# A graph network layer on one core: silu on ScalarE, and two kinds of tiles taken off GpSimd's gathers

## The chip, the cores and the metric

The kernel runs on one core of one Trainium2 chip. The metric is the device time of one execution in microseconds. The engines are called by the profile's names: PE (TensorE), DVE (VectorE), ACT (ScalarE), POOL (GpSimd) and SP (SyncE).

## The reference

There are 12500 nodes of 64 features and 412500 edges of 32 features, sorted by receiver (`dst`).

```
h = maximum(layernorm(x), 0)
m = concat(h[src], h[dst], edge_attr)                 # 160 wide, one row an edge
messages   = silu(m @ W1 + b1) @ W2 + b2              # 64 wide
att_logits = silu(m @ Wa1 + ba1) @ Wa2 + ba2          # one number an edge
att        = softmax(att_logits, axis=0)              # over all edges
agg        = segment_sum(messages * att, dst)
out        = x + silu(concat(h, agg) @ Wu1 + bu1) @ Wu2 + bu2
```

## The kernel before

**Tiles.** Edges are cut into tiles of 128 (`EP`), and 8 tiles (`K`) make a group; there are 403 groups (`NG`). The products of the first layers are split in three: a table `ts_d` in device memory holds, for each node as a sender, its 128 values (64 for the attention, 64 for the message); a table `tr_d` holds the same for receivers with the biases; the edge's own part is multiplied on PE. All of them are held at half size (the weights are halved), so that `tanh` of the sum gives `silu` of its double: silu(2z) = z (1 + tanh z).

**One group.** `load(g)` starts the fetches: for each tile one indirect DMA on POOL (L513) gathers the 128 senders' rows of `ts_d` into the tile `gs`; two DMAs on SP (L534) fetch a window of `tr_d` into one of three `wins`; each fourth group SP also fetches edges and receivers' numbers (`eo`, `dbs`). DVE compares the receivers' numbers (L538), and PE multiplies (L542) into the PSUM tile `pe`, 128 x 8 x 128. `begin(g)` adds `pe` and `gs` on DVE (L553) into `gs` and takes tanh on ACT (L556). `end(g)` multiplies on DVE: message (L566), attention (L572), times `wa2` (L574), and sums to a logit for each edge (L577). Four groups form a batch; `top` and `weigh` take the batch's largest logit, keep the running maximum `nmax`, and make the weights `p` with Exp on ACT (L610) and the correction `scale` of older sums with a second Exp (L607). `by_node(g)` builds for each tile a 128 x 40 matrix of weights by receiver (L620, eight instructions a group), PE sums messages with it (L626), ACT copies the sums out (`out_of`, L632), PE projects them (L637), and `put` adds them to the running sums at the window's place (L651, L655, L658).

**Columns.** In every second group from 8 to 390 (`EVERY`, 192 groups) the last tile isn't gathered. The nodes' features lie transposed on the chip (`hT`), and ACT copies, one instruction an edge, the 4-byte column of each of the 128 senders (L483) at an address taken from a register; `burst(g, k)` does 32 of them twice a group, each after a load of 32 registers (L479). `columns` writes `cols`, L547 masks the wrong half by the node's parity (`half`, fetched by SP), and one more product on PE (L548) adds the tile into `pe`.

**Order.** The loop over `g` runs `begin(g)`, parts of the summing up of a group five before (`sum_up`), `burst(g, 0)`, `load(g + 2)`, `numbers(g + 6)`, more summing up, `end(g)`, `burst(g, 1)`, and, where a batch begins, `weigh` of the batch before. `pin` puts an instruction behind the one traced before it on its engine; the register loads of `columns` and of `put` aren't pinned. In the groups 16 to 118 the loop also makes the nodes' own share of the last layer (`tile_bias`, L314 and L323; `tile_rest`). Gathers have 7 buffers, `pe` has 3. The last 12 groups have no columns, and the last 7 are batches of one group.

Of the kernel before, what the change touches and what calls it, by code (L numbers as in the profile page):

```python
# [44 lines left out]
WIDE = 128  # L45
EPS = 1e-5
# [313 lines left out]
def one_pass(tc, n_edges, v):  # L360
# [17 lines left out]
    with ExitStack() as ctx:  # L378
# [43 lines left out]
        with tc.tile_pool(name="work2", bufs=2) as work2, \  # L422
                tc.tile_pool(name="small", bufs=3) as small, \
                tc.tile_pool(name="pre_ps", bufs=AHEAD + 1, space=PSUM) as pre_ps, \
                tc.tile_pool(name="one_ps", bufs=1, space=PSUM) as one_ps:
            pes, gss, lgs, ps_, psums, sps, pps, ees, mts, nums, cols = ({} for _ in range(11))
# [12 lines left out]
            chosen = {g: i for i, g in enumerate(picks)}  # L439
            hT8 = v["hT"].rearrange("d b p -> d (b p)").bitcast(U8)  # L440
            sets = [(i, min(P, len(picks) - i)) for i in range(0, len(picks), P)]
# [3 lines left out]
            def places():  # L445

                num, low, near = (small.tile([P, len(sets), EP], t, name=n, bufs=1)
                                  for t, n in ((I32, "num"), (I32, "low"), (F32, "near")))
                pin(nc.vector.memset(num, 0))
                for k, (i, n) in enumerate(sets):  # L450
                    e = (picks[i] * K + K - 1) * EP
                    nc.sync.dma_start(num[:n, k, :], bass.AP(
                        tensor=v["src_row"].tensor, offset=v["src_row"][:, e:].offset,
                        ap=[[EVERY * K * EP, n], [1, EP]]))
# [8 lines left out]
                for k, (i, n) in enumerate(sets):  # L463
                    nc.sync.dma_start(par_d[k * P:k * P + n, :], low[:n, k, :])
# [3 lines left out]
            def numbers(g):  # L468
                if g in chosen:
                    n = nums[g] = small.tile([P, EP], I32, name="half", bufs=3)  # L470
                    row = par_d[chosen[g]:chosen[g] + 1, :]
                    nc.sync.dma_start(n, bass.AP(tensor=row.tensor, offset=row.offset, ap=[[0, P], [1, EP]]))
                    cols[g] = small.tile([P, EP], F32, name="cols", bufs=3)

            def columns(g, first, n):
                if g not in chosen:
                    return
                to, i = cols[g].bitcast(U8), chosen[g]
                _, regs = nc.values_load_multi_w_load_instructions(  # L479
                    spots[i % P:i % P + 1, i // P, first:first + n], engines=[ENG.Activation],  # L480
                    min_val=HT_AT, max_val=HT_AT + 2 * NP - 4, skip_runtime_bounds_check_because=WHY)
                for i in range(n):
                    pin(nc.scalar.copy(to[:, 4 * (first + i):4 * (first + i) + 4],  # L483
                                       hT8[:, bass.ds(regs[i] - HT_AT, 4)]))

            def burst(g, k):
# [6 lines left out]
            tr_w = bass.AP(tensor=tr_d.tensor, offset=tr_d.offset,  # L493
                           ap=[[C, NP + WR - SHIFT], [SHIFT * C, 2], [1, C]])

            def registers(g, engine, at, base=base_sb, top=NP - 1):
                n = min(NQ, NG + (base is not base_sb) - g)
                _, regs = nc.values_load_multi_w_load_instructions(
                    base[0:1, g:g + n], engines=[engine], min_val=0, max_val=top,
                    skip_runtime_bounds_check_because=WHY)  # L500
                for i in range(n):
                    at[g + i] = regs[i]

            def load(g):

                t = g * K
                if g % NQ == 0:
                    registers(g, ENG.SP, at_sp)
                full = gather.tile([P, K, C], F32, name="gs")
                gs = gss[g] = full[:EP]  # L510
                for j in range(K - (g in chosen)):
                    rows = WIDE if j in (2, 3) else EP
                    nc.gpsimd.indirect_dma_start(  # L513
                        out=full[:rows, j, :], out_offset=None, in_=ts_d[:, :],
                        in_offset=bass.IndirectOffsetOnAxis(ap=src_full[:rows, t + j:t + j + 1], axis=0))
# [17 lines left out]
                for r in range(2):  # L533
                    nc.sync.dma_start(win[r * R:(r + 1) * R, :, r, :],  # L534
                                      tr_w[bass.ds(at_sp[g], R), :, :])
# [14 lines left out]
            def begin(g):  # L550

                n = K - (g in chosen)
                pin(nc.vector.tensor_tensor(gss[g][:, :n, :], pes[g][:, :n, :], gss[g][:, :n, :], ALU.add))  # L553
                if n < K:
                    pin(nc.vector.tensor_copy(gss[g][:, n, :], pes[g][:, n, :]))
                pin(nc.scalar.activation(pes[g], gss[g], AF.Tanh))  # L556

            def end(g, then=None):

                s = batch[g]  # L560
                if g == starts[s]:
                    lgs[s] = small.tile([EP, B * K], F32, name="lg")
                gs, th = gss.pop(g), pes.pop(g)

                def message():
                    pin(nc.vector.scalar_tensor_tensor(acts[g % ACTS][:, :, 0:U], th[:, :, U:C], 1.0,  # L566
                                                       gs[:, :, U:C], op0=ALU.add, op1=ALU.mult))

                if g < NG - 1:
                    message()  # L570
                att = th[:, :, 0:U]
                pin(nc.vector.scalar_tensor_tensor(att, th[:, :, 0:U], 1.0, gs[:, :, 0:U],  # L572
                                                   op0=ALU.add, op1=ALU.mult))
# [3 lines left out]
                pin(nc.vector.tensor_reduce(lgs[s][:, k:k + K], att, AX.X, ALU.add))  # L577
# [4 lines left out]
                if g == NG - 1:  # L582
                    message()

            def top(s):

                n = size[s] * K
                lg = lgs[s]
# [10 lines left out]
            def weigh(s):  # L599
# [5 lines left out]
                fall = small.tile([P, 1], F32, name="fall")  # L605
                pin(nc.vector.tensor_tensor(fall, nmax[:, s + 1:s + 2], nmax[:, s:s + 1], ALU.subtract))
                pin(nc.scalar.activation(scale[:, s:s + 1], fall, AF.Exp))  # L607
                p = ps_[s] = small.tile([EP, B * K], F32, name="p")
                psum = small.tile([EP, 1], F32, name="psum")
                pin(nc.scalar.activation(p[:, :n], lgs.pop(s)[:, :n], AF.Exp, bias=nmax[:EP, s + 1:s + 2],  # L610
                                         accum_out=psum))
                psums[s] = psum

            def by_node(g):

                k = (g - starts[batch[g]]) * K
                wt = work2.tile([EP, K, W], F32, name="wt")
                p = ps_[batch[g]]
                for j in range(K):
                    pin(nc.vector.tensor_scalar(wt[:, j, :], iota_w[:EP, j // H, :],  # L620
                                                dloc[:, g * K + j:g * K + j + 1],
                                                p[:, k + j:k + j + 1],
                                                op0=ALU.is_equal, op1=ALU.mult))
# [94 lines left out]
            for g in range(NG):  # L718
# [6 lines left out]
                begin(g)  # L725
                if more and g < NG - 1:
# [10 lines left out]
                if g + AHEAD < NG:  # L737
                    load(g + AHEAD)
                numbers(g + 6)
# [384 lines left out]
```

## Time and profile before

| | |
|---|---|
| runs | 3901.23, 3902.33, 3901.85 us; median 3901.85 |
| the profiled execution | 3904.89 us, span of its instructions 3903.1 us |
| busy share of the span | DVE 80%, ACT 76%, POOL 74%, PE 61% |
| mean granted clock of PE | 0.642 |
| indirect DMAs on POOL | 3032, 198.90 MB by that queue |
| DMA | 391.30 MB, mean 100 GB/s |

A row of a group reads: line, engine, operation, output <- inputs, shape, count | busy us in all, mean ns of one | idle us of the engine just ahead of them, and what ended most of it. "Issue" is idle time in which the engine waited for nothing that the profile shows. A row of a stretch reads: the stretch, its length, then for PE, PEld (weight loads), DVE, ACT and POOL the busy us and the count, then PE's clock, the DMA engines' share and GB/s; with one line alone it has one engine only. A row of one line's records reads: line, engine (with a q: its queue, for loads, register work and DMA issues), operation, count, then shortest, median and longest ns, and the first and last start in us.

### The profile page before, as it was taken

What the parts mean: (1) busy time and instruction counts of PE and PEld (TensorE: products, weight loads), DVE (VectorE), ACT (ScalarE), POOL (GpSimd) and SP (SyncE); (2) the same over time, 40 slices, a digit from 0 to 9 for tenths busy, and PEclk for the clock granted to TensorE, in tenths of its full rate; (3) what the DMA queues carried; (4) which work ended last, traced back from release to release, by engine and by line L of the source; (5) the groups of instructions that cost most, each with busy time, mean ns of one, the idle gap of its engine ahead of it and who ended that gap; (6) DMA issues with size and microseconds to landing.
All of it is one profiled execution on the core that took longest, in us unless ns stands there. A gap on an engine that the chain in (4) does not pass through costs nothing. (4 is left out here: it accounts for less than half of the span.)

```text
span 3903.1 us, 72226 instructions
## 1 busy us (share of the span) xinstructions
PE 2368.6 (61%) x11368; PEld 1927.2 (49%) x11368; DVE 3115.4 (80%) x8929; ACT 2954.1 (76%) x25797; POOL 2888.6 (74%) x3057
## 2 busy tenths in 40 slices
PE   6566656666666666665665656556565565555655
PEld 5454444454445554554444545445444454444545
DVE  6888787878788888887877877778777777877887
ACT  2887777777778888887877777878877878878712
POOL 3777777777777777777777777777777777777774
PEclk8766566666666657666666666666666666666666
DMA  7433334333433333333333333333333333333343
GB/s 280 114 104 94 102 100 106 94 104 99 107 93 97 97 97 91 94 97 94 87 97 85 97 93 89 97 86 97 93 88 97 86 96 91 90 97 86 95 116 86
DMA packets 228304, 391.30 MB, mean 100 GB/s; under 512 B 72369, under 2 KB 155762, under 8 KB 214770
## 3 DMA queue, kind: packets, MB, share of 16 engines
q0 software_dynamic: 97024, 198.90, 19.5%
q1 hardware_dynamic: 130802, 187.73, 17.9%
q14 instruction: 385, 3.15, 0.3%
q8 instruction: 93, 1.52, 0.2%
HBM read 360.52 MB, written 25.82 MB: 99 GB/s over the span
## 5 line engine op out<-in xcount | busy, mean ns | idle before, releaser
L513 POOL DMA_INDIRECT gs<-ts_d,src_sb x3032 | 2871.4, 947 | 973.1 <-issue 844.2
L483 ACT COPY cols<-hT 128x4 uint8 x24576 | 2415.5, 189 | 595.2 <-issue 594.2
L542 PE MATMUL pe<-wins,eo 128*128 128x256 f32 x3224 | 1470.7, 630 | 846.4 <-DVE eo L538 619.9
L542 PEld LDWEIGHTS pe<-wins,eo 128*128 128x128 f32 x3224 | 964.4, 316 | 1145.4 <-DVE eo L538 708.6
L620 DVE TENSOR_SCALAR wt<-iota_w,dloc,p 128x40 f32<-128x40 f32 x3224 | 726.9, 323 | 1.8
L553 DVE TENSOR_TENSOR gs<-pe,gs 128x1024 f32<-128x1024 f32 (+1 forms) x403 | 467.0, 1159 | 325.7 <-DMA gs<-ts_d,src_sb 303.3
L626 PE MATMUL sp<-wt,acts 128*65 128x40 f32 x6448 | 621.9, 268 | 4.6 <-DVE wt L620 3.5
L626 PEld LDWEIGHTS sp<-wt,acts 128*65 128x65 f32 x6448 | 586.0, 183 | 11.4 <-DVE wt L620 6.2
L556 ACT ACTIVATE pe<-gs 128x1024 f32<-128x1024 f32 x403 | 410.6, 1019 | 215.9 <-DVE gs L553 125.3
L637 PEld LDWEIGHTS mt<-ss,w2u 65*128 65x128 f32 x806 | 201.7, 281 | 330.4 <-issue 291.9
L637 PE MATMUL mt<-ss,w2u 65*128 65x40 f32 x806 | 183.7, 322 | 255.5 <-DVE gm L603 221.4
L566 DVE SCALAR_TENSOR_TENSOR acts<-pe,gs 128x512 f32<-128x512 f32 x403 | 277.6, 689 | 21.6 <-ACT pe L556 12.2
L574 DVE TENSOR_TENSOR pe<-pe,w_all 128x512 f32<-128x512 f32 x403 | 281.8, 699 | 13.5
L572 DVE SCALAR_TENSOR_TENSOR pe<-pe,gs 128x512 f32<-128x512 f32 x403 | 280.3, 696 | 10.5
L596 PE MATMUL mt<-ident,mx 128*128 128x128 f32 x107 | 46.7, 437 | 396.4 <-DVE sums L655 375.9
L577 DVE TENSOR_REDUCE lg<-pe 128x8 f32<-128x512 f32 x403 | 276.7, 687 | 10.5
L538 DVE TENSOR_SCALAR eo<-dbs,bj 64x256 f32<-64x256 int32 x806 | 275.5, 371 | 9.2
L596 PEld LDWEIGHTS mt<-ident,mx 128*128 128x128 f32 x107 | 19.2, 179 | 408.3 <-issue 404.5
L658 DVE COPY stand<-nmax 64x40 f32 x806 | 159.0, 197 | 3.4 <-issue 0.3
L547 DVE SCALAR_TENSOR_TENSOR cols<-half,cols 128x128 f32<-128x128 int32 x192 | 67.1, 349 | 100.6 <-ACT cols L483 98.5
L651 DVE SCALAR_TENSOR_TENSOR sums<-sums,scale,mt 64x40 f32 x214 | 54.4, 254 | 110.9 <-PE mt L637 107.4
L548 PEld LDWEIGHTS pe<-stack,cols 128*128 128x128 f32 x384 | 121.7, 317 | 32.5
(126 smaller groups left out, 957.6 us busy)
## 6 DMA issues: line engine op xcount, KB each, us to landing
eo<-in_edge_dram SPq DMA_DIRECT2D x100, 512.0 KB
dbs<-in_dst_row_dram SPq DMA_DIRECT2D x200, 256.0 KB
gs<-ts_d,src_sb POOLq DMA_INDIRECT x3032
wins<-tr_d SPq DMA_DIRECT2D x806, 32.0 KB
half<-par_d SPq DMA_DIRECT2D x192, 64.0 KB
ts_d<-ts SPq DMA_DIRECT2D x5, 896.0 KB
tr_d<-tr SPq DMA_DIRECT2D x5, 896.0 KB
hT_d<-hT SPq DMA_DIRECT2D x7, 448.0 KB
```

What stands on the lines that cost most here:

```text
L483: pin(nc.scalar.copy(to[:, 4 * (first + i):4 * (first + i) + 4], hT8[:, bass.ds(regs[i] - HT_AT, 4)]))
L513: nc.gpsimd.indirect_dma_start(out=full[:rows, j, :], out_offset=None, in_=ts_d[:, :], in_offset=bass.IndirectOffsetOnAxis(ap=src_full[:ro ...
L542: pin(nc.tensor.matmul(pe[:, 2 * q:2 * q + 2, :], eo[:, q * EP:(q + 1) * EP], win[:, q // 2, :, :], start=True, stop=q < H - 1 or g not in ...
L553: pin(nc.vector.tensor_tensor(gss[g][:, :n, :], pes[g][:, :n, :], gss[g][:, :n, :], ALU.add))
L556: pin(nc.scalar.activation(pes[g], gss[g], AF.Tanh))
L566: pin(nc.vector.scalar_tensor_tensor(acts[g % ACTS][:, :, 0:U], th[:, :, U:C], 1.0, gs[:, :, U:C], op0=ALU.add, op1=ALU.mult))
L572: pin(nc.vector.scalar_tensor_tensor(att, th[:, :, 0:U], 1.0, gs[:, :, 0:U], op0=ALU.add, op1=ALU.mult))
L574: pin(nc.vector.tensor_tensor(att, att, wa2[:EP, None, :].to_broadcast([EP, K, U]), ALU.mult))
L577: pin(nc.vector.tensor_reduce(lgs[s][:, k:k + K], att, AX.X, ALU.add))
L620: pin(nc.vector.tensor_scalar(wt[:, j, :], iota_w[:EP, j // H, :], dloc[:, g * K + j:g * K + j + 1], p[:, k + j:k + j + 1], op0=ALU.is_equ ...
L626: pin(nc.tensor.matmul(sp, acts[g % ACTS][:, j, :], wt[:, j, :], start=j == 0, stop=j == K - 1))
L637: pin(nc.tensor.matmul(pp, w2u.rearrange("s h u -> s (h u)"), sps.pop(g), start=True, stop=True))
```

## The change

- `begin(g)` adds the gathered rows into `pe` in PSUM, and ACT makes silu(2z) from there with two instructions, one for the attention half into a tile `att` and one for the message half straight into `acts`. The two products on DVE (L566, L572) go, and so does the copy of the column tile out of PSUM.
- Exp isn't used in the loop any more. `weigh` makes the weights from Tanh: with t = tanh(x/32), ((1 + t)/(1 - t)) = exp(x/16); three squarings on DVE give exp(x/2), and Square on ACT with its accumulator gives exp(x) and the sum. The correction `scale` rides along as a 33rd column.
- `by_node` builds the eight matrices of a group in two instructions (one comparison, one product of 128 x 320).
- In every eighth group (11, 19, ... 387: 48 groups) the last tile's columns are copied by DVE: `vcolumns` loads eight registers twice a group, `spare_columns` issues the copies, 16 a group, so that a tile takes eight groups.
- In every eighth group (15, 23, ... 383: 47 groups) the last tile is fetched row by row by SP: `fetch` loads 16 registers and issues 16 DMAs of 512 bytes a group; the byte addresses are the senders' numbers shifted left by 9 on DVE, and `begin` adds the tile `lone` with an addition of its own.
- The windows' addresses are given in bytes (`base_by`), shifted once ahead of the loop.

```diff
+ROWS = 16
+ROW0 = 6
+VTURN = 8
+VRES = (3,)
+VSTART = 0
+VLATER = 11
+VBUFS = 2
...
+            vpicks = [g for g in range(VSTART + VLATER, NG - 12) if g % VTURN in VRES]
...
+            def vcolumns(g, part):
+                at, end = (i * EP * len(VRES) // (2 * VTURN) for i in (2 * (g - VSTART) + part,
+                                                                        2 * (g - VSTART) + part + 1))
+                end = min(end, len(vpicks) * EP)
+                while 0 <= at < end:
+                    t, first = vpicks[at // EP], at % EP
+                    n = min(end - at, EP - first)
+                    if first == 0:
+                        cols[t] = small.tile([P, EP], F32, name="vcols", bufs=VBUFS)
+                    loads, regs = spots_of(t, first, n, ENG.DVE)
+                    for one in loads:
+                        pin(one)
+                    to = cols[t].bitcast(U8)
+                    waiting.extend((to[:, 4 * (first + i):4 * (first + i) + 4], regs[i]) for i in range(n))
+                    at += n
+
+            def spare_columns(n=None):
+                for to, reg in waiting[:n]:
+                    pin(nc.vector.tensor_copy(to, hT8[:, bass.ds(reg - HT_AT, 4)]))
+                waiting[:] = waiting[len(waiting) if n is None else n:]
...
+            for i in range(NG):
+                g = ROW0 + (EP * (i + 1) - 1) // ROWS + 2
+                if g < NG - 12:
+                    fetched[g] = i
...
+            def fetch(g):
...
+                    loads, regs = nc.values_load_multi_w_load_instructions(
+                        ids[i][0:1, first:first + n], engines=[ENG.SP], min_val=0, max_val=(NP - 1) * 4 * C,
+                        skip_runtime_bounds_check_because=WHY)
+                    for one in loads:
+                        pin(one)
+                    for k in range(n):
+                        pin(nc.sync.dma_start(to[first + k:first + k + 1, :].bitcast(U8),
+                                          ts8[bass.ds(regs[k], 4 * C)][None, :]))
...
-                for j in range(K - (g in chosen)):
+                for j in range(K - (g in chosen) - (g in fetched)):
...
-                n = K - (g in chosen)
-                pin(nc.vector.tensor_tensor(gss[g][:, :n, :], pes[g][:, :n, :], gss[g][:, :n, :], ALU.add))
-                if n < K:
-                    pin(nc.vector.tensor_copy(gss[g][:, n, :], pes[g][:, n, :]))
-                pin(nc.scalar.activation(pes[g], gss[g], AF.Tanh))
+                n = K - (g in chosen) - (g in fetched)
+                pe, gs = pes[g], gss.pop(g)
+                pin(nc.vector.tensor_tensor(pe[:, :n, :], pe[:, :n, :], gs[:, :n, :], ALU.add))
+                if g in fetched:
+                    pin(nc.vector.tensor_tensor(pe[:, n, :], pe[:, n, :], lone.pop(g)[:EP], ALU.add))
+                del pes[g]
+                att = atts[g] = silus.tile([P, K, U], F32, name="att")[:EP]
+                pin(nc.scalar.activation(att, pe[:, :, 0:U], AF.Silu, scale=2.0))
+                pin(nc.scalar.activation(acts[g % ACTS][:, :, 0:U], pe[:, :, U:C], AF.Silu, scale=2.0))
...
-                pin(nc.scalar.activation(scale[:, s:s + 1], fall, AF.Exp))
+                lg = lgs.pop(s)
+                pin(nc.vector.tensor_scalar(lg[:, n:n + 1], nmax[:, s:s + 1], -1.0, None, op0=ALU.mult))
+                part = small.tile([P, 1], F32, name="part")
+                pin(nc.vector.tensor_scalar(part, nmax[:, s + 1:s + 2], 1.0 / 32, None, op0=ALU.mult))
+                t, d = (small.tile([P, B * K + 1], F32, name=k)[:, :n + 1] for k in ("t", "d"))
+                pin(nc.scalar.activation(t, lg[:, :n + 1], AF.Tanh, bias=part, scale=1.0 / 32))
+                spare_columns()
+                pin(nc.vector.tensor_scalar(d, t, -1.0, 1.0, op0=ALU.mult, op1=ALU.add))
+                spare_columns(3)
+                pin(nc.vector.reciprocal(d, d))
+                spare_columns(3)
+                pin(nc.vector.scalar_tensor_tensor(t, t, 1.0, d, op0=ALU.add, op1=ALU.mult))
+                for _ in range(3):
+                    spare_columns(3)
+                    pin(nc.vector.tensor_tensor(t, t, t, ALU.mult))
                 p = ps_[s] = small.tile([EP, B * K], F32, name="p")
                 psum = small.tile([EP, 1], F32, name="psum")
-                pin(nc.scalar.activation(p[:, :n], lgs.pop(s)[:, :n], AF.Exp, bias=nmax[:EP, s + 1:s + 2],
-                                         accum_out=psum))
+                pin(nc.scalar.activation(p[:, :n], t[:EP, :n], AF.Square, accum_out=psum))
+                spare_columns(3)
+                pin(nc.vector.tensor_tensor(scale[:, s:s + 1], t[:, n:n + 1], t[:, n:n + 1], ALU.mult))
...
-                for j in range(K):
-                    pin(nc.vector.tensor_scalar(wt[:, j, :], iota_w[:EP, j // H, :],
-                                                dloc[:, g * K + j:g * K + j + 1],
-                                                p[:, k + j:k + j + 1],
-                                                op0=ALU.is_equal, op1=ALU.mult))
+                at = dloc[:, g * K:(g + 1) * K].rearrange("p (r h) -> p r h", h=H)
+                pin(nc.vector.tensor_tensor(wt.rearrange("p (r h) w -> p r h w", h=H),
+                                            iota_w[:EP, :, None, :].to_broadcast([EP, 2, H, W]),
+                                            at[:, :, :, None].to_broadcast([EP, 2, H, W]), ALU.is_equal))
+                pin(nc.vector.tensor_tensor(wt, wt, p[:, k:k + K, None].to_broadcast([EP, K, W]), ALU.mult))
...
                 begin(g)
+                vcolumns(g, 0)
...
                     load(g + AHEAD)
+                fetch(g)
                 numbers(g + 6)
...
+                spare_columns()
+                vcolumns(g, 1)
                 end(g)
                 burst(g, 1)
                 if batch[g] and g == starts[batch[g]]:
                     weigh_upto(batch[g] - 1)
+                spare_columns()
```

More of the change, by code (lines that the diff above doesn't have):

```diff
@@ L488, in burst @@
                     columns(g + 3 + i, *SLOTS[EVERY - 1 - i][k])
-            at_sp, at_lo, at_hi, bus, rest = {}, {}, {}, {}, {}
[L493 to L497, printed above, removed]
+            fetched = {}
+            for i in range(NG):
+                g = ROW0 + (EP * (i + 1) - 1) // ROWS + 2
+                if g < NG - 12:
+                    fetched[g] = i
@@ new lines, in one_pass, with ask, scaled @@
+            order = list(fetched)
+            ids, lone = {}, {}
+            ts8 = ts_d.rearrange("n f -> (n f)").bitcast(U8)
+            def ask(i):
+                if i < len(order):
+                    g = order[i]
+                    e = (g * K + K - 1 - (g in chosen)) * EP
+                    ids[i] = small.tile([1, EP], I32, name="ids", bufs=2)
+                    nc.sync.dma_start(ids[i], v["src_row"][:, e:e + EP])
+            def scaled(i):
+                if i < len(order):
+                    pin(nc.vector.tensor_scalar(ids[i], ids[i], 9, None, op0=ALU.logical_shift_left))
@@ new lines, in fetch @@
+            def fetch(g):
+                at = (g - ROW0) * ROWS
+                end = min(at + ROWS, len(order) * EP)
+                if g == ROW0 - 3:
+                    ask(0)
+                if g == ROW0 - 2:
+                    scaled(0)
+                while 0 <= at < end:
+                    i, first = at // EP, at % EP
+                    n = min(end - at, EP - first)
+                    if first < ROWS:
+                        ask(i + 1)
+                    if EP // 2 <= first < EP // 2 + ROWS:
+                        scaled(i + 1)
+                    if first == 0:
+                        lone[order[i]] = small.tile([P, C], F32, name="lone", bufs=2)
+                    to = lone[order[i]]
+                    loads, regs = nc.values_load_multi_w_load_instructions(
[6 more added lines that the diff above has]
+                                          ts8[bass.ds(regs[k], 4 * C)][None, :]))
+                    at += n
@@ new lines, in one_pass, with registers @@
+            at_sp, at_lo, at_hi, bus, rest = {}, {}, {}, {}, {}
+            row = 4 * C
+            tr8 = tr_d.bitcast(U8)
+            tr_w = bass.AP(tensor=tr8.tensor, offset=tr8.offset,
+                           ap=[[1, (NP - 1) * row + 1], [row, R], [SHIFT * row, 2], [1, row]])
+            base_by = keep.tile([1, NG + 1], I32, name="base_by")
+            nc.vector.tensor_scalar(base_by[:, :NG], base_sb[:, :NG], 9, None, op0=ALU.logical_shift_left)
+            def registers(g, engine, at, base, top):
+                n = min(NQ, NG + (base is not base_by) - g)
@@ L561, in end @@
                 if g == starts[s]:
[L562 to L573, printed above, removed]
+                    lgs[s] = small.tile([P, B * K + 1], F32, name="lg")
+                    if EP < P:
+                        pin(nc.vector.memset(lgs[s][P - R:], 0.0))
+                att = atts.pop(g)
                 pin(nc.vector.tensor_tensor(att, att, wa2[:EP, None, :].to_broadcast([EP, K, U]),
```

55 lines of the change are left out of this document (29 added, 26 removed).

## The prediction

> **What bounds the kernel now.** I read the page's busy shares and groups first, then the waits, then the records of one line.
>
> ```profile
> PE 2368.6 (61%) x11368; PEld 1927.2 (49%) x11368; DVE 3115.4 (80%) x8929; ACT 2954.1 (76%) x25797; POOL 2888.6 (74%) x3057
> ...
> L513 POOL DMA_INDIRECT gs<-ts_d,src_sb x3032 | 2871.4, 947 | 973.1 <-issue 844.2
> L483 ACT COPY cols<-hT 128x4 uint8 x24576 | 2415.5, 189 | 595.2 <-issue 594.2
> ...
> L620 DVE TENSOR_SCALAR wt<-iota_w,dloc,p 128x40 f32<-128x40 f32 x3224 | 726.9, 323 | 1.8
> L553 DVE TENSOR_TENSOR gs<-pe,gs 128x1024 f32<-128x1024 f32 (+1 forms) x403 | 467.0, 1159 | 325.7 <-DMA gs<-ts_d,src_sb 303.3
> ...
> L556 ACT ACTIVATE pe<-gs 128x1024 f32<-128x1024 f32 x403 | 410.6, 1019 | 215.9 <-DVE gs L553 125.3
> ...
> L566 DVE SCALAR_TENSOR_TENSOR acts<-pe,gs 128x512 f32<-128x512 f32 x403 | 277.6, 689 | 21.6 <-ACT pe L556 12.2
> ...
> L572 DVE SCALAR_TENSOR_TENSOR pe<-pe,gs 128x512 f32<-128x512 f32 x403 | 280.3, 696 | 10.5
> ```
>
> No engine is full, but POOL's idle time is mostly its own "issue". The records of the gather line and two neighbours on the timeline:
>
> ```profile
> L513 POOL DMA_INDIRECT gs<-ts_d,src_sb x3032: 940/944/1352, 51.7 to 3846.0; - x190
> ...
> 2002.14 0.94 POOL L513 DMA_INDIRECT gs<-ts_d,src_sb  x1 [0.30 <-issue]
> 2003.39 0.95 POOL L513 DMA_INDIRECT gs<-ts_d,src_sb  x1 [0.30 <-issue]
> ```
>
> From 51.7 to 3846.0 us there are 3031 steps, so 1.2518 us a gather, exactly the spacing of the two rows. POOL never pauses: **the count of gathers sets the time**. Groups have 8 or 7 gathers, 7.5 on average: 9.39 us a group. The others have little in hand. How fast do they go when POOL is ahead? Stretches of the span, all engines and then line L556 alone (one per group), with their largest waits:
>
> ```profile
> 1000.00:2000.00 1000.00, 632.01 (x3013) 511.70 (x3012) 822.13 (x2384) 822.20 (x7364) 756.46 (x800) 0.63 0.37 95
> 2500.00:3500.00 1000.00, 586.43 (x2894) 481.45 (x2894) 789.71 (x2292) 796.26 (x7100) 756.50 (x800) 0.63 0.35 92
> ...
> 200.00:1000.00 800.00, 83.53 (x82) 0.62 0.38 101
> 1000.00:2000.00 1000.00, 111.80 (x110) 0.63 0.37 95
> ...
> DVE bu L323 <- PE mt L314: 82.1, 20, 4.5
> ...
> ACT cols L483 <- issue: 157.9, 220, 1.1
> ```
>
> In 200 to 1000 the compute ran at 800/82 = 9.76 us a group, behind POOL, with 82.1 us of VectorE waiting for the tile biases; POOL used its buffers to stay busy. In 1000 to 2000 it caught up at 9.09. ScalarE's need there, busy plus loading registers, is (822.2 + 157.9)/110 = **8.91 us a group**. That is the second bound, 5% under the first.
>
> **POOL, removed.** One fetched tile in eight groups (47 in all) and one VectorE tile in eight (48) take away 95 gathers: 95 x 1.2518 = 118.9 us. Against the profiled execution's 3904.89 us (median of the runs 3901.85) that leaves a floor of **3786**; the pace becomes 58 gathers in 8 groups, 9.075 us.
>
> **ScalarE.** Rows for an activation of 512 elements from PSUM, for one weighing among the columns, and for a register load:
>
> ```profile
> L239 ACT COPY ts<-pn 128x512 f32<-128x512 f32 x22 | 12.8, 589 | 10.2 <-PE pn L237 8.3 <-DMA ts_d<-ts 1.4 <-ACT ts L239 0.2
> ...
> 2060.93 3.14 ACT L483 COPY cols<-hT 128x4 uint8 x32 [0.28 <-issue]
> 2065.00 3.14 ACT L483 COPY cols<-hT 128x4 uint8 x32 [0.92 <-issue]
> 2068.05 0.20 ACT L607 ACTIVATE scale<-fall 128x1 f32<-128x1 f32 x1
> 2068.15 0.31 ACT L610 ACTIVATE p<-lg,nmax 128x32 f32<-128x32 f32 x1
> 2068.36 0.19 ACT L610 ACTIVATION_READ_ACCUMULATOR p<-lg,nmax 128x1 f32 x1
> ...
> L479 ACTq TENSOR_LOAD <-spots x768: 1942/2008/2800, 98.4 to 3706.6; - x192
> ```
>
> Two silus replace one tanh of 1.019. Columns last 0.189 but follow at 3.14/32 = 0.098, so neighbours overlap by 0.09: 2 x 0.589 - 0.09 = 1.09, +0.07 a group (bounds 0 and +0.16). The trace has no silu; I take the copy's time. A weighing has two activations as before, one of 33 columns in place of one: +0.05 per four groups. Need: 8.91 + 0.07 + 0.01 = 8.99, under POOL's 9.075.
>
> The new wait: between Tanh and Square stand six dependent VectorE steps, and the next group's addition follows behind them on VectorE. Rows of such steps:
>
> ```profile
> 2058.59 0.18 DVE L655 TENSOR_TENSOR sums<-sums,mt 64x40 f32 x1
> 2058.69 0.18 DVE L658 COPY stand<-nmax 64x40 f32 x1
> ...
> 2065.26 0.16 DVE L604 TENSOR_TENSOR nmax<-gm,nmax 128x1 f32<-128x1 f32 x1
> 2065.46 0.16 DVE L606 TENSOR_TENSOR fall<-nmax 128x1 f32<-128x1 f32 x1
> ```
>
> Dependent steps follow at 0.20; the operands are 33 wide and one is a reciprocal, so six take about 1.3 us (an estimate from these rows). Then the scale (0.2) and the next addition (1.2) before the next silu may start: 2.7, of which ScalarE fills 0.4 with Square and the accumulator. So a weighing costs between 0 and 2.3 us of ScalarE per four groups; queued behind Square are the next silus and their columns. It is 0 if the next burst's loads and columns are put into the gap. The trace bears that out in part: gaps ahead of a burst are 0.28 where its 2.0 us load went ahead of the tanh and 0.92 where it didn't. I take 0.6, the exposed rest of a load: pace 8.99 + 0.15 = 9.14.
>
> **VectorE.** 789.71 us of 1000 at 9.39 is 7.4 a group. Away: the two products, (277.6 + 280.3)/403 = 1.38, and eight comparisons, 8 x 726.9/3224 = 1.80. In their place two operations of 320 elements:
>
> ```profile
> L275 DVE TENSOR_TENSOR tr<-pn,w_all 128x512 f32<-128x512 f32 x22 | 14.5, 688 | 10.0 <-DMA tr_d<-tr 6.7 <-PE pn L273 3.2
> ...
> L275 DVE TENSOR_TENSOR tr<-pn,w_all 128x256 f32<-128x256 f32 x5 | 2.1, 415 | 0.0
> ```
>
> By these 0.48 each, 0.97. The addition now lands in PSUM, as L572's product did in 0.696 beside L566's 0.689 into SBUF: nothing; it frees the gather's buffer at once and the PSUM buffer after the silus, before the logits instead of after them, which can only help POOL and TensorE. A weighing gains eight steps net, 0.4 a group. Without columns: 5.6. Sixteen columns cost 0.10 each (L655 to L658, neighbours that don't depend) to 0.18 (no overlap): 1.6 to 2.9; I take 1.6, since they don't depend on each other. Their two loads of eight:
>
> ```profile
> L498 DVEq TENSOR_LOAD <-bases x202: 336/343/600, 142.4 to 3853.0; - x101
> L498 SPq TENSOR_LOAD <-base_sb x101: 294/301/753, 87.2 to 3774.6; - x101
> ...
> L148 SPq DMA_DIRECT2D base_sb<-in_first_dram x1: 307/307/307, 7.8 to 7.8; - x1
> ...
> L534 SPq FUSED_REGOPS  x806: 37/37/51, 88.1 to 3808.6; - x162
> L534 SPq MOVE wins<-tr_d x806: 29/29/38, 88.1 to 3808.6; - x162
> L534 SPq DMA_DIRECT2D wins<-tr_d x806: 316/317/1870, 88.2 to 3808.7; - x162
> ...
> L472 SPq DMA_DIRECT2D half<-par_d x192: 344/367/551, 94.8 to 3660.9; - x192
> ```
>
> 343 ns for four and 2008 for 32 make 59.5 a register: 0.58 each, under the 1.2 us addition and under eight columns, so hidden; uncovered 1.16 a group. Once in eight groups there is a 128x128 addition of the fetched tile, one scaling of its numbers and one comparison for VectorE's own tile, below 0.1 a group together; the copy of the columns' tile out of PSUM goes away and pays for them. VectorE: 7.2, at worst 9.7, against 9.14: if its cover (waiting for ScalarE) is gone, the columns show in full.
>
> **SyncE.** A group gets 16 single fetches: one row took 0.307, with address work 0.37 to 0.43, so 5.9 to 6.9, and a load of 16 registers, 0.301 + 12 x 0.0595 = 1.0. The two windows (0.77), the numbers and the four-group loads (about 0.5) make 8.2 to 9.2, taken 8.4. It is in order and stops at each window until TensorE frees it, three groups ahead of use; that slack is the cover for the windows, the edges and the number rows queued behind the fetches. Were SyncE above the pace, TensorE's first products of a group would wait for a window, and VectorE's addition for them. The fetched rows themselves land two groups before they are added.
>
> **Sum.** Early region: VectorE is 0.2 lighter and its bias waits stay, so about 9.5 for some 105 groups: (9.5 - 9.075) x 105 = 45 us behind POOL. Some 270 further groups at 9.14: +18. The last dozen groups have no columns and 8 gathers, 10.0 us. The tail of before, all engines and then line L553 alone:
>
> ```profile
> 3720.00:3845.00 125.00, 72.90 (x402) 59.66 (x401) 104.13 (x331) 19.38 (x53) 94.50 (x101) 0.65 0.41 120
> ...
> 3720.00:3845.00 125.00, 15.77 (x13) 0.65 0.41 120
> ```
>
> VectorE needs 104.13/13 = 8.0 there; less 1.38 and 0.83, plus 1.6 for a weighing in each group and its wait for Tanh, it is about 8.3, and a dozen groups take back 20. Result 3786 + 43 = **3829 us**.
>
> **A page that speaks against it.** POOL's gathers stayed at 947 against a least of 940 while VectorE ran L620 eight times a group: 7 ns x 3032 = 21 us in all, so I charge the copies nothing. The Trainium skill's "SBUF — State Buffer", section "Who interferes with whom", says that a VectorE copy in a two-port mode blocks GpSimd for its whole length. By it, 48 x 128 copies of 0.10 could cost some 600 us; the 7 ns do not bear that out.
>
> **Rivals.**
> - *POOL alone* (0.17). ScalarE fills the gaps and catches up: 3786, or 3778 to 3795, since gathers at their least, 940, would give up to 2937 x 0.007 = 21 us more, of which I count a part. For it: 8.99 is under 9.075.
> - *The weighing stalls ScalarE* (0.21), the case on the other side. At 2.3 the pace is 9.57: 45 + 134, some 30 more early, less 20, gives 3975; it decides from 1.7 per weighing on (9.42: 45 + 93 - 20, 3904). For it: bursts in the trace stay whole. Against: loads do move.
> - *SyncE sets the pace* (0.08): at 9.28, lag 79 - 20, 3845; with stops at windows up to 3900.
> - *VectorE sets it* (0.06): columns at 0.18 and open loads, 9.7: 3786 + 240 - 20 = 4006.
> - *Silu and Tanh don't share a table* (0.03), so that the change buys a switch at each weighing. The loop now loads one table:
>
> ```profile
> L556 ACT ACT_TABLE_LOAD x1: 1283/1283/1283, 97.7 to 97.7; - x1
> ```
>
>   Outside the loop Exp then needs one load more at the end, 1.3 us, and the larger list of tiles a few DMAs before the loop, behind POOL's first gathers; both are inside the forecast's rounding. In the loop two switches a weighing add 2.57/4 = 0.64 a group, 9.78: 45 + 190, some 20 more early, less 20, 4021. The Trainium skill's "ScalarE: Activation LUTs", section "Table sets: the hidden batching unit", gives each set one expensive anchor and lists tanh beside exp and beside sigmoid; no run here shows silu's set.
>
> **Numbers.** The forecast, ScalarE and POOL near a tie with a small stall, has 0.45: 3788 (no stall) to 3870 (1.2 a weighing). Low end 3778 is POOL alone; high end 3960 takes in SyncE and over half of the stall, leaving out nearly 0.2. Measurement tells 0.2% (8 us). Faster: 0.45 + 0.17 + 0.06 less a little, 0.67; same 0.05; slower 0.28.
>
> **What would show it.** 2937 gathers at 1.25 us with short pauses only; silus near 0.59; Square's wait on VectorE under 0.6; VectorE columns at 0.10; windows never late. I am wrong if POOL pauses for whole groups, or if ScalarE waits over 1.7 us per weighing.

## The result: 3.2% slower, and the profile after

The changed kernel takes **4027.8 us** (median of 4 runs, 4025.44 to 4029.11) against 3902.09 (4 runs, 3901.23 to 3902.96) of the kernel before: a ratio of 1.032, 95% interval 1.0307 to 1.0333. The forecast was 3829, with a range of 3778 to 3960: wrong in sign, and the result lies outside the range. It went the way of the rival "The weighing stalls ScalarE". The profiled execution took 4025.44 us, with a span of 4023.7.

From the page of the changed kernel, busy shares and groups:

```profile
PE 2281.7 (57%) x11464; PEld 1843.6 (46%) x11464; DVE 2853.9 (71%) x12656; ACT 2971.1 (74%) x26201; POOL 2895.0 (72%) x2962
...
L602 POOL DMA_INDIRECT gs<-ts_d,src_sb x2937 | 2877.8, 980 | 1071.1 <-issue 819.3
L498 ACT COPY cols<-hT 128x4 uint8 x24576 | 2415.8, 189 | 546.6 <-issue 545.4
...
L521 DVE COPY vcols<-hT 128x4 uint8 x6144 | 551.0, 194 | 22.3 <-issue 22.1
L643 DVE TENSOR_TENSOR pe<-pe,gs 128x896 f32<-128x896 f32 (+1 forms) x403 | 457.8, 1136 | 32.4 <-issue 19.8
...
L648 ACT ACTIVATE att<-pe 128x512 f32<-128x512 f32 x403 | 237.7, 590 | 218.1 <-DVE pe L643 215.0
...
L659 DVE TENSOR_TENSOR att<-att,w_all 128x512 f32<-128x512 f32 x403 | 276.4, 686 | 40.2 <-ACT att L648 37.1
```

VectorE fell from 3115 to 2854 us of work, and 95 gathers went as the change says. No engine became busier in share; all of them wait more. Two numbers stand out. A gather has a mean of 980 ns where it had 947, and the first silu (L648) waits 215.0 us for VectorE's addition. The waits of the same kernel (engine, line, waited for: us in total, times, longest) give two more, and the records of the gathers show that they no longer run without a pause:

```profile
POOL gs L602 <- DVE pe L643: 153.7, 90, 3.0
...
ACT p L705 <- DVE t L702: 169.1, 106, 3.2
```

```profile
L602 POOL DMA_INDIRECT gs<-ts_d,src_sb x2937: 938/944/1465, 51.0 to 3950.3; - x196
```

From 51.0 to 3950.3 a gather takes 3899.3/2936 = 1.328 us: 0.980, the usual 0.30 between two, and 0.05 of pauses, the 153.7 us above, in which POOL has no free buffer. Now the timeline of ScalarE through four groups, shortened to the lines that carry the argument:

```profile
2606.50 0.32 ACT L693 ACTIVATE t<-lg,part 128x33 f32<-128x33 f32 x1
2608.39 0.23 ACT L705 ACTIVATE p<-t 128x32 f32<-128x32 f32 x1 [1.57 <-DVE t L702]
2610.03 0.60 ACT L648 ACTIVATE att<-pe 128x512 f32<-128x512 f32 x1 [1.31 <-DVE pe L643]
...
2619.41 0.59 ACT L648 ACTIVATE att<-pe 128x512 f32<-128x512 f32 x1
...
2620.78 3.14 ACT L498 COPY cols<-hT 128x4 uint8 x32 [0.24 <-issue]
...
2627.97 0.59 ACT L648 ACTIVATE att<-pe 128x512 f32<-128x512 f32 x1
...
2645.11 0.32 ACT L693 ACTIVATE t<-lg,part 128x33 f32<-128x33 f32 x1
...
2650.77 0.38 ACT L498 COPY cols<-hT 128x4 uint8 x3 [0.97 <-issue]
```

From one weighing Tanh (L693) to the next are 38.61 us, 9.65 a group, where before had 9.39. A group without a weighing takes only 2627.97 - 2619.41 = 8.56. So four groups without a stall would be 34.2; the weighing's own activations and the rest of a load (0.97 where 0.24 would do) add about 1.4, and **1.57 + 1.31 = 2.88 us is ScalarE idle twice inside one weighing**: Square waits for the six steps on VectorE, and the next silu waits for the addition queued behind them. VectorE in the same moment:

```profile
2606.86 0.18 DVE L695 TENSOR_SCALAR d<-t 128x33 f32<-128x33 f32 x1 [4.19 <-ACT t L693]
2607.07 0.37 DVE L697 RECIPROCAL d<-d 128x33 f32<-128x33 f32 x1
2607.47 0.20 DVE L699 SCALAR_TENSOR_TENSOR t<-t,d 128x33 f32<-128x33 f32 x1
2607.70 0.65 DVE L702 TENSOR_TENSOR t<-t 128x33 f32<-128x33 f32 x3
2608.39 0.16 DVE L707 TENSOR_TENSOR scale<-t 128x1 f32<-128x1 f32 x1
2608.76 1.23 DVE L643 TENSOR_TENSOR pe<-pe,gs 128x1024 f32<-128x1024 f32 x1 [0.21 <-issue]
```

VectorE stood idle 4.19 us ahead of the chain, with the addition's inputs long there: it waits for Tanh, then ScalarE waits for it. Neither is busy enough to be the bound; the order in which they hand over is.

### The profile page after: what moved, and what is told of

It is laid out like the page before. It is cut to its first block, busy times and chain, and to the rows that moved or that the text cites. A ratio compares the mean times of both kernels' runs of the same rounds, so it can differ in the third digit from the quotient of the medians.

```text
span 4023.7 us, 87496 instructions
## 1 busy us (share of the span) xinstructions
PE 2281.7 (57%) x11464; PEld 1843.6 (46%) x11464; DVE 2853.9 (71%) x12656; ACT 2971.1 (74%) x26201; POOL 2895.0 (72%) x2962
## 3 DMA queue, kind: packets, MB, share of 16 engines
q1 hardware_dynamic: 149968, 194.05, 18.8%
## 5 line engine op out<-in xcount | busy, mean ns | idle before, releaser
L498 ACT COPY cols<-hT 128x4 uint8 x24576 | 2415.8, 189 | 546.6 <-issue 545.4
L631 PE MATMUL pe<-wins,eo 128*128 128x256 f32 x3224 | 1344.8, 589 | 1163.4 <-DVE eo L627 1117.8
L521 DVE COPY vcols<-hT 128x4 uint8 x6144 | 551.0, 194 | 22.3 <-issue 22.1
L643 DVE TENSOR_TENSOR pe<-pe,gs 128x896 f32<-128x896 f32 (+1 forms) x403 | 457.8, 1136 | 32.4 <-issue 19.8
L648 ACT ACTIVATE att<-pe 128x512 f32<-128x512 f32 x403 | 237.7, 590 | 218.1 <-DVE pe L643 215.0
L659 DVE TENSOR_TENSOR att<-att,w_all 128x512 f32<-128x512 f32 x403 | 276.4, 686 | 40.2 <-ACT att L648 37.1
L662 DVE TENSOR_REDUCE lg<-att 128x8 f32<-128x512 f32 x403 | 274.9, 682 | 10.6
L649 ACT ACTIVATE acts<-pe 128x512 f32<-128x512 f32 x403 | 234.7, 582 | 0.0
L719 DVE TENSOR_TENSOR wt<-wt,p 128x320 f32<-128x320 f32 x403 | 198.9, 493 | 13.9
L716 DVE TENSOR_TENSOR wt<-iota_w,dloc 128x320 f32<-128x320 f32 x403 | 197.3, 490 | 1.6
L637 PE MATMUL pe<-stack,cols 128*128 128x128 f32 x384 | 105.6, 364 | 84.7 <-DVE cols L636 83.7
```

The lines of the kernel that those rows point to most:

```text
L521: pin(nc.vector.tensor_copy(to, hT8[:, bass.ds(reg - HT_AT, 4)]))
L631: pin(nc.tensor.matmul(pe[:, 2 * q:2 * q + 2, :], eo[:, q * EP:(q + 1) * EP], win[:, q // 2, :, :], start=True, stop=q < H - 1 or g not in ...
L643: pin(nc.vector.tensor_tensor(pe[:, :n, :], pe[:, :n, :], gs[:, :n, :], ALU.add))
L648: pin(nc.scalar.activation(att, pe[:, :, 0:U], AF.Silu, scale=2.0))
L649: pin(nc.scalar.activation(acts[g % ACTS][:, :, 0:U], pe[:, :, U:C], AF.Silu, scale=2.0))
L662: pin(nc.vector.tensor_reduce(lgs[s][:EP, k:k + K], att, AX.X, ALU.add))
```

## The experiments

Theory **W**: the time is set by that hand-over, because Tanh, Square and the next silu follow each other directly on ScalarE. Rival **G**: the longer gathers (980 for 947 ns) hold the kernel up. Each ratio is against the kernel before, run beside it on the same chip (medians 3910.01, then 3902.18, then 3902.28), with its 95% interval.

**Split the weighing.** Tanh is issued ahead of the next burst of 32 columns, Square behind it, so the chain has a burst to run beside (`weigh_a` goes through the three squarings, `weigh_b` makes Square and the scale):

```diff
                 end(g)
+                early = batch[g] and g == starts[batch[g]] and weighed[0] == batch[g] - 1
+                if early:
+                    weigh_a(batch[g] - 1)
                 burst(g, 1)
-                if batch[g] and g == starts[batch[g]]:
+                if early:
+                    weigh_b(batch[g] - 1)
+                    weighed[0] += 1
+                elif batch[g] and g == starts[batch[g]]:
                     weigh_upto(batch[g] - 1)
```

> The changed kernel, but in the loop Tanh is issued ahead of the group's second burst of columns on ScalarE and Square behind it, so that VectorE's steps between them run beside the burst. Theory W (each weighing stops ScalarE for 1.57 us at Square and 1.31 us at the next silu, and all else follows): the four-group cycle falls from 38.6 by 2.9 to 35.7 us, under POOL's 29 gathers of 0.980 + 0.303 = 37.2 us, so POOL sets the time: about 51 + 2937 x 1.283 + 73 = 3892 us, 3880 to 3905. Theory G (the gathers, 980 ns here against 947 before, set the time of the changed kernel): no change, 4015 to 4035.

Measured 3893.38 us (3889.28 to 3898.92), 0.9955 [0.9939, 0.9972]. ScalarE's timeline, a wait of VectorE and the gathers of this kernel:

```profile
2626.43 0.32 ACT L699 ACTIVATE t<-lg,part 128x33 f32<-128x33 f32 x1
2628.17 3.14 ACT L498 COPY cols<-hT 128x4 uint8 x32 [1.42 <-issue]
2631.22 0.22 ACT L716 ACTIVATE p<-t 128x32 f32<-128x32 f32 x1
...
DVE pe L643 <- DMA gs<-ts_d,src_sb: 335.9, 137, 7.1
...
L602 POOL DMA_INDIRECT gs<-ts_d,src_sb x2937 | 2890.9, 984 | 946.8 <-issue 849.8
L602 POOL DMA_INDIRECT gs<-ts_d,src_sb x2937: 943/947/1542, 53.3 to 3839.2; - x196
```

Here Square waits for nothing; in the whole run its wait for VectorE falls from 169.1 us to 18.8. The ratio falls from 1.032 to 0.9955, some 142 us, and it is VectorE that now waits for gathers: POOL is the bound again, at 3785.9/2936 = 1.2895 us. W holds for the slowdown. But with 95 gathers fewer the kernel should have gained 119 us and gained 17: the gathers' extra 37 ns (984 - 947) times 2937, 109 us, take that back. G names the second half of the loss: it is the bound that comes next, and in the changed kernel the weighing's wait lies above it.

**Put the first silu back into PSUM,** so that its product with the weights has one SBUF operand, alone and together with the split:

```diff
-                att = atts[g] = silus.tile([P, K, U], F32, name="att")[:EP]
+                att = atts[g] = pe[:, :, 0:U]
```

> The changed kernel, but the attention half's silu is written back into PSUM instead of into SBUF, so that the product with wa2 on VectorE has one input in PSUM as in the kernel before. Theory G: gathers fall back to some 950 ns and with them the time by 2937 x 0.03, some 90 us, to 3935. Theory W: gathers fall back to some 950 ns, and the time stays, 4010 to 4035, with longer pauses on POOL for buffers. If it is the VectorE copies of the columns that slow the gathers, they stay at 980.

> Both edits at once: Tanh and Square on the two sides of the second burst, and the attention half in PSUM. W and G as two bounds, one behind the other: POOL at 1.25 a gather gives 51 + 2937 x 1.252 + 73 = 3801 us, or some tens more where ScalarE's 8.9 us a group lags in the early groups: 3795 to 3840, faster than before. If only W is true and gathers don't matter: as e1. If neither: 4025.

Measured 4433.41, 1.1339 [1.132, 1.1358], and with the split 4114.5, 1.0523 [1.0506, 1.0541]. Both expectations missed. From the first of these kernels, ScalarE's wait, its timeline and the gathers:

```profile
ACT cols L497 <- issue: 917.9, 767, 1.7
...
2022.13 0.57 ACT L647 ACTIVATE pe<-pe 128x512 f32<-128x512 f32 x1
2022.73 0.60 ACT L648 ACTIVATE acts<-pe 128x512 f32<-128x512 f32 x1
...
2024.84 3.14 ACT L497 COPY cols<-hT 128x4 uint8 x32 [1.43 <-issue]
...
L601 POOL DMA_INDIRECT gs<-ts_d,src_sb x2937 | 2819.2, 960 | 1533.0 <-issue 875.0
```

Gathers fell to 960 ns (962 with the split), as G wants, but the time didn't follow: "issue" ahead of the columns is 917.9 us where it was 545.4. The second silu reads the tile that the first now writes; the two no longer overlap (0.60 apart, 0.49 before), and the gap ahead of the columns became 1.43 where it was 0.24. The records of ScalarE's queue show why: the load of 32 registers starts here at 2022.74, with the second silu, and in the changed kernel at 2618.67, 0.74 us ahead of the first. So the load was held up until the second silu could run. That it is the shared tile that held it is my reading; no run isolated it. The pair therefore decides nothing between W and G.

**Lengthen the chain** by six steps that multiply by 1:

```diff
                     pin(nc.vector.tensor_tensor(t, t, t, ALU.mult))
+                for _ in range(6):
+                    pin(nc.vector.tensor_scalar(t, t, 1.0, None, op0=ALU.mult))
```

> The changed kernel with six further dependent VectorE steps (times 1.0, 128x33) between Tanh and Square, the suspected wait about doubled. Theory W: 6 x 0.2 = 1.2 us more in each of some 96 weighings beside columns: 4130 to 4150. Theory G: POOL has slack nowhere in this, the wait is hidden: 4020 to 4045.

Measured 4182.22, 1.0697 [1.0679, 1.0715]; the wait of Square in this kernel:

```profile
ACT p L707 <- DVE t L704: 306.4, 102, 4.2
```

3.00 us a wait for 1.60. The ratio rose from 1.032 to 1.0697, some 147 us or 1.4 for each of 107 weighings: each step of the chain is paid in full. W, somewhat above its 4130 to 4150 (the kernel before, too, took 8 us more on this chip); G's number is missed by 137 us and more.

**The weighing alone,** put into the kernel before (`...` marks what is left out):

```diff
-                pin(nc.scalar.activation(scale[:, s:s + 1], fall, AF.Exp))
+                pin(nc.scalar.activation(t, lg[:, :n + 1], AF.Tanh, bias=part, scale=1.0 / 32))
+                ...                     # the six steps on VectorE
-                pin(nc.scalar.activation(p[:, :n], ..., AF.Exp, ..., accum_out=psum))
+                pin(nc.scalar.activation(p[:, :n], t[:EP, :n], AF.Square, accum_out=psum))
```

> The kernel before with one part of the change alone: the weighing by Tanh, six VectorE steps and Square in place of two Exp. Theory W: ScalarE's need of 8.91 us a group, 35.6 in four, plus a wait of 2.9 makes a cycle of 38.6 us against POOL's 30 gathers, 37.55: about 96 x 1.05 = 100 us more, 3980 to 4010. If the wait alone were harmless and only harms together with silu and the VectorE columns: 3895 to 3915.

Measured 4166.79, 1.0678 [1.066, 1.0696]. ScalarE's timeline, and its gathers:

```profile
2620.38 0.23 ACT L618 ACTIVATE p<-t 128x32 f32<-128x32 f32 x1 [1.72 <-DVE t L615]
...
2622.01 1.03 ACT L556 ACTIVATE pe<-gs 128x1024 f32<-128x1024 f32 x1 [1.31 <-DVE gs L553]
...
L513 POOL DMA_INDIRECT gs<-ts_d,src_sb x3032 | 2869.4, 946 | 1183.4 <-issue 1028.2
```

The same two waits, 3.03 us, with gathers at their old 946: the weighing alone costs 265 us, and the rest of the change, added to it, wins back 139 (4166.79 to 4027.8). It came out over 150 us above the expectation, which had counted only what the wait adds above POOL's pace. By the starts of L556, 136 us are lost up to group 118 already, some 4.6 a batch. In that region the compute was behind POOL before the change too (9.76 us a group), so there a wait is not covered by any slack. That a batch loses more there than the 3.03 of the two waits is not explained by any run; the size stays open.

**The gathers by themselves.** In the kernel before, the product ahead of the attention weights is written to SBUF instead of PSUM, so that the next one (L575) has two SBUF operands, as in the change; the sum behind it (L578) then reads SBUF as well:

```diff
-                att = th[:, :, 0:U]
+                att = silus.tile([P, K, U], F32, name="att")[:EP]
```

> The kernel before with one edit: the product that L572 makes goes to a tile in SBUF, so that the product with wa2 that follows has both inputs in SBUF, as in the changed kernel. Theory G2 (a VectorE instruction with two SBUF inputs holds up the gather beside it, in the changed kernel by about 200 ns each time): 403 such products put some 88 us on POOL, gathers go from 947 to some 975 ns, and as POOL sets the time of this kernel: 3980 to 3995. If the VectorE columns slow the gathers: gathers stay at 947 and the time at 3895 to 3915.

Measured 3966.9 (3961.35 to 3966.93), 1.0161 [1.0144, 1.0178]. VectorE and POOL on the timeline, and the gathers:

```profile
2000.32 0.68 DVE L575 TENSOR_TENSOR att<-att,w_all 128x512 f32<-128x512 f32 x1
...
2000.48 1.34 POOL L514 DMA_INDIRECT gs<-ts_d,src_sb  x1 [0.30 <-issue]
2002.13 0.94 POOL L514 DMA_INDIRECT gs<-ts_d,src_sb  x1 [0.30 <-issue]
...
L514 POOL DMA_INDIRECT gs<-ts_d,src_sb x3032 | 2934.4, 968 | 971.9 <-issue 868.3
```

The gather that runs beside L575 takes 1.34, the next one 0.94. The mean rises by 21 ns; 21 ns x 3032 = 64 us, and the time rose by 65. So 403 such products cost about 65/403 = 0.16 us each. The time stayed below the expected 3980 to 3995, so the size was over-expected; the mechanism is there. The records say which instruction does it, and when. After the first 200 us, 222 gathers begin while L575 runs, and they take 0.27 us more than the median of 0.944 on average. The 250 that had begun before it stay within 0.01 of the median, and so do the 124 that begin while L578 runs. In the kernel before, 211 gathers begin beside the same product, there with one input in PSUM, and on average they stay at that median. The changed kernel shows it too, L659 beside a gather:

```profile
2621.41 0.69 DVE L659 TENSOR_TENSOR att<-att,w_all 128x512 f32<-128x512 f32 x1
...
2621.54 1.39 POOL L602 DMA_INDIRECT gs<-ts_d,src_sb  x1 [0.30 <-DMA gs<-ts_d,src_sb]
```

The Trainium skill's "SBUF — State Buffer", section "Who interferes with whom", says that a VectorE instruction with two SBUF inputs contends with a GpSimd instruction that reads SBUF. The trace agrees: the one gather here is delayed by 0.45 us, nearly all of the 0.56 that it lies beside the product. But not each product delays one: of 63 in the changed kernel between 2000 and 2600 us, worked out from the records, 33 have a gather beside them that takes over 1 us, since a gather has to begin while the product runs. That is why the mean is only 0.16.

**Two cures on top of the split.** First the eight comparisons of before in place of the two products of 320 (the diff is that of the change, undone); then the attention half of silu and the weights in bf16, which shortens their product and rounds these numbers (one line of the edit; the weights become the bf16 tile `wa2b`):

```diff
-                att = atts[g] = silus.tile([P, K, U], F32, name="att")[:EP]
+                att = atts[g] = silus.tile([P, K, U], BF16, name="att")[:EP]
```

> As e1_split, but by_node is made as in the kernel before, with eight comparisons of one SBUF tensor each in place of two instructions of 320 elements with two. G2: these two instructions hold up gathers too, with some 70 to 90 ns beside them: gathers 10 to 15 ns shorter, 3893 less 30 to 45, 3848 to 3865. If only the product with wa2 does it: gathers at 984 and 3885 to 3900. VectorE's 0.8 us more a group should not show, since it waited 336 us for gathers.

> As e1_split, but the attention half's silu and wa2 are bf16, so that the product with wa2 still reads two tensors from SBUF but may take about half of its 0.69 us. G2: the hold-up shrinks with the length of the instruction, gathers fall from 984 to 950 to 965 ns and the time with them, 3815 to 3855. If the length doesn't matter, or the product isn't what holds gathers up: 984 and 3885 to 3900.

Measured 3857.23, 0.9883 [0.9866, 0.9899], and 3839.35, 0.9839 [0.9822, 0.9855]. From the second, the product and the gathers:

```profile
L662 DVE TENSOR_TENSOR att<-att,wa2b 128x512 bf16<-128x512 bf16 x403 | 168.9, 419 | 18.6 <-issue 13.5
L605 POOL DMA_INDIRECT gs<-ts_d,src_sb x2937 | 2832.8, 965 | 946.5 <-issue 853.5
```

The product takes 419 ns for 686, and gathers 965 for 984; with the comparisons they take 971. Both land in the expected ranges.

**All three, the second cure without the split, and all three with half as many fetched tiles** (ROWS 16 to 8: 23 fetched, 24 more gathers):

> Three edits at once on the changed kernel: Tanh and Square on the two sides of the second burst, by_node with the eight comparisons of before, attention half in bf16. W and G2 together: gathers at some 952 ns and POOL without pauses, 53 + 2937 x 1.256 + 58 = 3800 us, 3795 to 3825, the fastest so far. Theory S (SyncE's single fetches, which wait for older transfers, now hold the windows and through them TensorE): 3830 to 3850 with over 200 us of TensorE's waits for windows.

> The changed kernel with the attention half in bf16 alone; Tanh and Square stay next to each other. It takes the place of e2_psum as the test of the gathers alone. W: gathers fall from 980 to some 960 ns, and the time stays, 4010 to 4035, with longer pauses of POOL for buffers. G: the time falls with the gathers, by 2937 x 0.02, some 60 us, 3960 to 3975.

> As e11_all, but SyncE fetches 8 rows a group instead of 16: 23 tiles in place of 47, so 2961 gathers. If POOL sets e11_all: 24 gathers more, 24 x 1.256 = 30 us slower than it. If S: SyncE is relieved, and it is as fast as e11_all or faster.

Measured 3814.32 (3811.99 to 3817.62), 0.9773 [0.9756, 0.9789]; 4022.45, 1.0309 [1.0292, 1.0326]; 3848.84, 0.9856 [0.9839, 0.9872]. The gathers of the first with two waits of TensorE, and the gathers of the second with its wait of the first silu and POOL's for a buffer:

```profile
L605 POOL DMA_INDIRECT gs<-ts_d,src_sb x2937 | 2810.7, 957 | 946.4 <-issue 860.1
...
PE pe L634 <- DMA wins<-tr_d: 346.0, 88, 8.9
PE pe L634 <- DMA lone<-ts_d: 153.4, 43, 6.7
```

```profile
L605 POOL DMA_INDIRECT gs<-ts_d,src_sb x2937 | 2838.8, 967 | 1106.1 <-issue 843.5
...
ACT att L651 <- DVE pe L646: 210.6, 132, 6.1
POOL gs L605 <- DVE pe L646: 177.2, 94, 3.0
```

The middle one parts the two theories: gathers faster by 13 ns, time unchanged to 0.2%, and POOL waits for buffers longer instead, 177.2 us for 153.7. While the weighing stalls ScalarE, these 13 ns win nothing. Once it is split, most of each ns of a gather is paid 2937 times: by the ratios the two cures and both together win 28, 45 and 71 us, where 13, 19 and 27 ns make 38, 56 and 79. All three edits together beat both kernels, by 2.3% the one before. There POOL still sets the time: 24 gathers more cost 34.5 us, 1.4 each, about what a gather takes. The sign that theory S had asked for did appear, over 200 us of TensorE's waits for windows (346.0). But with half the fetches these waits fall to 17.7, and the kernel is slower, so they do not set the time.

## Why the prediction was wrong

- **The failed step is the weighing's wait.** The prediction bounded it by 0 and 2.3 us and took 0.6, "the exposed rest of a load", on the thought that loads and columns move into the gap. They don't: nothing stands between Tanh, Square and the silus in the written order, and the load for the next burst doesn't move either. In the group shown it starts at 2610.11 by the queue's records, only when the waiting silu has been let go at 2610.03; so it is in 120 groups whose silu waited, where the load starts 0.08 us behind the silu; in 262 others it starts 0.74 us ahead. Measured 2.88, plus 0.73 for the load behind it, past the upper bound, since Square's own wait (1.57, the chain being 1.5 and not 1.3) and the addition (1.31) are both paid. The rival priced at 3975 was this mechanism; its condition, over 1.7 us, is met.
- **The pace.** Sized 9.14 us a group, measured 9.65: 0.51 x 270 groups = 138 of the 196 us that separate 3829 from 4025.44. The weighing takes 3.61/4 = 0.90 a group where 0.15 was taken; the other 0.24 went the other way, since ScalarE's rest is 8.75 for 8.99. The rest is in the early region. Stretches of line L648 alone, one per group, of the changed kernel and then of the split one:

```profile
200.00:1000.00 800.00, 45.56 (x77) 0.63 0.38 96
```

```profile
200.00:1000.00 800.00, 49.80 (x85) 0.62 0.42 101
```

  800/77 = 10.4 against the 9.5 forecast costs 77 x 0.9 = 69; split, it is 9.4, so the early term was right but for the same stall. The two estimates together come to 207, 11 over.
- **ScalarE without the stall** was right and better: silu 0.590 where 0.589 was taken, and 8.56 a group without a weighing against a need of 8.99 that has some 0.1 of weighing in it, since a load is hidden behind two silus but for 0.24.
- **POOL: the count right, the duration wrong.** "I charge the copies nothing" holds: in the kernel with all three edits 6144 VectorE columns remain, and gathers are 957 against a median of 944; that excess, 13 ns x 2937 = 38 us, is what 403 products of 419 ns cost at 0.16 us per 0.686 (39 us). No run took the columns away, but the records bear it out: in the changed kernel 350 gathers after the first 200 us lie beside copies and beside none of the products nor the sum behind them (L662), and they are 1 ns over the median. But the search for interference stopped at the copies: the new two-SBUF products (L659, L716, L719) were costed on VectorE alone, as POOL's floor of 3786 shows. That floor is 3893 in the split kernel.
- **VectorE** was right to below: products of 320 at 0.49 for 0.48, the addition into PSUM at 1.14 for 1.16, eight columns 0.66 to 0.70, 0.08 each for 0.10.
- **SyncE** was over-sized:

```profile
L571 SPq MOVE lone<-ts_d x6016: 29/29/38, 120.4 to 3778.5; - x195
L571 SPq DMA_DIRECT2D lone<-ts_d x6016: 224/228/305, 120.5 to 3778.5; - x195
L565 SPq TENSOR_LOAD <-ids x376: 972/1168/1332, 119.4 to 3772.3; - x188
```

  A single fetch is 0.26, not 0.37 to 0.43, and a load of 16 registers 1.17 for 1.0: 16 x 0.257 + 1.17 = 5.3 us a group where the prediction had 6.9 to 7.9. Windows are late for 26.4 us in all here, and for 346.0 in the kernel with all three edits, where the rest is faster; "windows never late" did not hold there.
- **The table rival** falls: silu and tanh run from the one table loaded ahead of the loop.

```profile
L648 ACT ACT_TABLE_LOAD x1 | 1.3, 1283 | 48.7 <-DVE pe L643 48.7
```

## What to carry to other kernels

A helper chain that leaves an in-order engine and comes back is paid in full, with what is queued behind it on the other engine, unless the written order puts independent work between the two halves; look at the order of issue before believing that a gap fills itself, and at whether register loads still run ahead when the instruction in front of them waits. When one engine's count of equal instructions sets the time, ask of every new instruction on the other engines what it does to the duration of that one, operand by operand: where its inputs lie can matter more than its own cost.

## What was not expected of the hardware

A VectorE product of 128x512 with both inputs in SBUF lengthened the gathers that began while it ran, in the case shown from 0.94 to 1.39 us, by 0.16 us on average per product; gathers that had begun before it kept their time, and the same product with one input in PSUM left gathers at 947. And where two activations followed each other on one PSUM tile, the first writing it, the next load of registers started only with the second, and ScalarE's gap ahead of the next columns was 1.43 us for 0.24.
